# Inverse roots on VectorE instead of ScalarE, and small products moved into a bank of scores

## The chip, the cores and the metric

The kernel runs on one core of one Trainium2 chip. The metric is the device time of one execution in microseconds (us). All data is float32.

## The reference

The input is `x` of 8 images, 256 channels, 64 x 64 pixels. Two layers are applied, each on a group-normalised `x` (32 groups of 8 channels, mean and variance over the group's channels and all pixels) and each added to `x`:

```python
def _gn(v, G=32, eps=1e-5):
    g = v.reshape(B_, G, C_ // G, H_, W_)
    m = jnp.mean(g, axis=(2, 3, 4), keepdims=True)
    s = jnp.var(g, axis=(2, 3, 4), keepdims=True)
    return ((g - m) / jnp.sqrt(s + eps)).reshape(v.shape)
x = x + layer0(_gn(x))
x = x + layer1(_gn(x))
```

Layer 0 makes three 1x1 convolutions, runs two of them through batch norms, ReLUs and two more 1x1 convolutions to nine weights per pixel and group, and sums the third over a 3x3 neighbourhood with those weights. Layer 1 is half an attention over a 7x7 neighbourhood in 4 heads (with a position term and softmax) and half a sum of nine depthwise convolutions weighted by a softmax over nine. An inverse square root is needed once for the batch norms and twice for each image, for the group norm of each layer.

## The kernel before

An image is cut into 8 bands (i = 0 to 7) of 8 rows. A loop over `g` (64 bands of layer 1) has 8 steps `s` in each turn. A turn computes layer 1 on band `g`, and beside it layer 0 on band `g + 12`, so that TensorE, VectorE (DVE), ScalarE (ACT) and GpSimd (POOL) all work through a queue of instructions whose order is written out by hand under `tc.manual_schedule()`. Twelve turns with `g < 0` come first; they have layer 0 alone.

In each step the function `advance()` is called six times, and `after(n, f)` puts `f` behind the n-th call from now. I call these places 1 to 6 of a step:

- Before place 1: in even steps the scores of two tiles of the attention (L736, into the tile `sco`), the weighted values of the steps before (L785, into the tile `small`) and a transpose (`ptp`, L773). In every step then `masked` (VectorE, L750, reads `sco`, writes the negative maximum `nmax`), `add_values` (L804) and the exponentials (ScalarE, L758).
- Between places 1 and 2: the first product `pf` of the convolution weights (L872) with its exponential `ex` (L877), in odd steps a transpose, and two depthwise taps on VectorE (L829 or L855).
- Between 2 and 3: `probabilities` (VectorE L765, ScalarE L767) and the matmuls of `mid`: queries (L670), keys (L692), values (L594) or layer 0's maps (L369).
- Between 3 and 4: what follows these matmuls. For keys that is the additions L700 and L707 on VectorE; in step 3 of most bands they belong to the second half of the channels, of which the scores of step 4 are made. Then more taps.
- Between 4 and 5: the second `pf` and `ex`. Between 5 and 6: `end`, among it layer 0's tap weights `pw` (L464), whose products on VectorE (L477) come one and two places later and are added up on GpSimd (L485). GpSimd also adds the two `ex` (L1087).

TensorE's results are in eight banks of 512 columns: a score tile takes two (one per head of a pair; a step pair uses 2 x 196 = 392 columns of each), `small` one, `acc` one, and the other four rotate under the tag `gen`, one bank for each tile, however narrow.

`small` is shared: weighted values are written to its columns 0 to 255 (`po = home[:, : 2 * P]`), and layer 0's small maps (L328) or hidden products (L428) to columns from 256 on (`p12 = home[:, 2 * P :]`).

The group norms are done by `gn_affine`, a chain of functions a1 to a6 that follow each other by `after`. Per-channel means and variances come from `bn_aggr`; a first small matmul (L237) averages the means over each group (`pg`), a2 (L246, L249, L250) turns that into `d`, a second matmul averages `d`, and from that come the scale `sc` (inverse root) and the shift `bi` (L269). It is used twice:

- `scaled_weights` (below: event a), called in step 2 of the band i = 3, for the layer 0 of the next image. It scales the weights on ScalarE (`scale`, L296 and L297) and makes bias products `pb` (`through`, L304) that `biases` adds up.
- `norm_rows` (event b), called in step 2 of the band i = 6, for the layer 1 of the next image. It copies scale and shift (`keep`), spreads them over channels by four small matmuls (`by_channel`, L542, tile `pgc`), and `take` (L547) copies the result.

For images 0 and 1 (event a) and 0 (event b) this is in the turns with `g < 0`; six events a and seven events b are in the turns with `g >= 0`. The last event b is in a turn with no layer 0 beside it.

In terms of step and place, event a goes: a1 at 2/3, a2 at 2/5, a3 at 3/4, a4 (L258) at 3/6, a5 (the square root on ScalarE, L262) at 4/2, a6 and `scale` at 4/6, `through` at 5/5, `biases` at 6/1. Event b is the same up to a6 with `keep`; `by_channel` follows at 5/3 and `take` at 5/5.

Of the kernel before, what the change touches and what calls it, by code (L numbers as in the profile page):

```python
# [9 lines left out]

F32 = mybir.dt.float32
BF16 = mybir.dt.bfloat16
AF = mybir.ActivationFunctionType
ALU = mybir.AluOpType
AX = mybir.AxisListType
# [3 lines left out]
P = 128  # L19
C = 256  # L20
NCT = C // P
# [5 lines left out]
GN_EPS = 1e-5  # L27
BN_EPS = 1e-5
# [26 lines left out]
NKEY = KW * KW  # L55
CHUNK = R * KW
NPROB = 2 * CHUNK
NEG = -1.0e30


AHEAD = NB + 4
# [25 lines left out]
def conv_layers_kernel(ctx: ExitStack, tc: tile.TileContext, ins: dict, out: bass.AP):  # L87
    nc = tc.nc
# [3 lines left out]
    const = ctx.enter_context(tc.tile_pool(name="const", bufs=1))  # L92
# [14 lines left out]
    def load(name, shape, src=None, now=True):  # L107
        t = const.tile(shape, F32, name=f"c_{name}")
        late.append(lambda: nc.scalar.dma_start(out=t, in_=ins[name] if src is None else src))
        if now:  # L110
            late.pop()()
        return t

    gmat = load("gmat", [P, P])
    par = load("par", [P, NPAR])
# [24 lines left out]
    for t in probs + x3n + h2n:  # L140
        nc.gpsimd.memset(t, 0.0)

    def rstd_(out_, var, eps):
        nc.vector.tensor_scalar(out_, var, eps, None, ALU.add)
        nc.scalar.activation(out_, out_, AF.Sqrt)
        nc.vector.reciprocal(out_, out_)


    bn1s = const.tile([P, 3], F32, name="bn1s")
    bn1b = const.tile([P, 3], F32, name="bn1b")  # L150
    bn2s = const.tile([P, 1], F32, name="bn2s")
    bn2b = const.tile([P, 1], F32, name="bn2b")
    for s, t, g, b_, m, v, n, p in (
        (bn1s, bn1b, PG, PB, PM, PV, 3, P),
        (bn2s, bn2b, PG2, PB2, PM2, PV2, 1, P),
    ):
        rstd_(s, par[:p, v : v + n], BN_EPS)
        nc.vector.tensor_mul(s, s, par[:p, g : g + n])
        nc.vector.tensor_mul(t, s, par[:p, m : m + n])
        nc.vector.tensor_sub(t, par[:p, b_ : b_ + n], t)  # L160
# [19 lines left out]
    stat = ctx.enter_context(tc.tile_pool(name="stat", bufs=2))  # L180
    w0 = ctx.enter_context(tc.tile_pool(name="l0", bufs=2))
    w1 = ctx.enter_context(tc.tile_pool(name="l1", bufs=2))
    ps = ctx.enter_context(tc.tile_pool(name="ps", bufs=1, space=PSUM))
# [31 lines left out]
    def after(n, f):  # L215
        later.append((place[0] + n, f))

    def advance():
# [3 lines left out]
        for f in ready:  # L222
            f()

    def gn_affine(sts, means, name, done):


        n = len(sts)
        mv = stat.tile([P, n, 2], F32, name=f"mv_{name}", tag=f"mv{n}")
        for ct, st in enumerate(sts):  # L230
            nc.vector.bn_aggr(mv[:, ct, :], st)
        mean, var = mv[:, :, 0], mv[:, :, 1]
        gm, d, sc, bi = (stat.tile([P, n], F32, name=f"{v}_{name}", tag=f"{v}{n}") for v in ("gm", "d", "sc", "bi"))

        def group_means(v, k):
            pg = ps.tile([P, n], F32, name=f"pg_{name}_{k}", tag="gen", bufs=4)
            nc.tensor.matmul(pg, means, v, start=True, stop=True)  # L237
            return pg


        def a1():
            pg = group_means(mean, 0)
            after(2, lambda: a2(pg))

        def a2(pg):
            nc.vector.tensor_copy(gm, pg)  # L246
            for ct in range(n):
                c = slice(ct, ct + 1)
                nc.vector.tensor_scalar(d[:, c], pg[:, c], mean[:, c], None, ALU.subtract)  # L249
                nc.vector.tensor_scalar(d[:, c], d[:, c], d[:, c], var[:, c], ALU.mult, ALU.add)  # L250
            after(5, a3)

        def a3():
            pg = group_means(d, 1)
            after(2, lambda: a4(pg))

        def a4(pg):
            nc.vector.tensor_scalar(sc, pg, GN_EPS, None, ALU.add)  # L258
            after(2, a5)

        def a5():
            nc.scalar.activation(sc, sc, AF.Sqrt)  # L262
            after(4, a6)

        def a6():
            nc.vector.reciprocal(sc, sc)
            for ct in range(n):
                c = slice(ct, ct + 1)
                nc.vector.tensor_scalar(bi[:, c], gm[:, c], sc[:, c], -1.0, ALU.mult, ALU.mult)  # L269
            done(sc, bi)  # L270

        after(3, a1)


# [13 lines left out]
    def scaled_weights(b):  # L288

        im = images[b]  # L290

        def scale(sc, bi):
            im.w12s = w0.tile([P, NCT, 2 * REL], F32, tag="w12s", name=f"w12s_{b}", bufs=1)
            im.w3s = w0.tile([P, NCT, C], F32, tag="w3s", name=f"w3s_{b}", bufs=1)
            for kt in range(NCT):
                nc.scalar.activation(im.w12s[:, kt], w12[:, kt], AF.Copy, scale=sc[:, kt : kt + 1])  # L296
                nc.scalar.activation(im.w3s[:, kt], w3[:, kt], AF.Copy, scale=sc[:, kt : kt + 1])  # L297
            after(5, lambda: through(bi))

        def through(bi):  # L300
            pb = ps.tile([P, 1 + NCT], F32, tag="gen", name=f"pb_{b}", bufs=4)
            for m, to, w in ((0, 0, w12), (0, 64, w12), (1, 0, w3[:, :, :P]), (2, 0, w3[:, :, P:])):
                for kt in range(NCT):
                    nc.tensor.matmul(  # L304
                        pb[to : to + w.shape[2], m : m + 1], w[:, kt], bi[:, kt : kt + 1],
                        start=(kt == 0), stop=(kt == NCT - 1),
                    )
            after(2, lambda: biases(pb))

        def biases(pb):  # L310
            im.bias = w0.tile([P, 1 + NCT], F32, tag="bias", name=f"bias_{b}")
            nc.vector.tensor_add(im.bias[:, 0:1], pb[:, 0:1], par[:, PB21 : PB21 + 1])
            for ct in range(NCT):
                nc.vector.tensor_add(
                    im.bias[:, 1 + ct : 2 + ct], pb[:, 1 + ct : 2 + ct], chan[:, ct, CB3 : CB3 + 1]
                )

        gn_affine([im.st0[:, ct] for ct in range(NCT)], gmat, f"a{b}", scale)

    def small_maps(b, i, home):  # L320
# [208 lines left out]
    def norm_rows(b):  # L529
        im = images[b]  # L530


        def keep(sc, bi):
            both = stat.tile([P, 2], F32, name=f"both_{b}", tag="both")
            nc.vector.tensor_copy(both[:, 0:1], sc)
            nc.vector.tensor_copy(both[:, 1:2], bi)
            after(3, lambda: by_channel(both))

        def by_channel(both):
            pg = ps.tile([P, NCT, 2], F32, tag="gen", name=f"pgc_{b}", bufs=4)  # L540
            for ct in range(NCT):
                nc.tensor.matmul(pg[:, ct], gc[:, ct], both, start=True, stop=True)  # L542
            after(2, lambda: take(pg))

        def take(pg):
            im.aff = stat.tile([P, NCT, 2], F32, name=f"aff_{b}", tag="aff")
            nc.vector.tensor_copy(im.aff, pg)  # L547

        gn_affine([im.st1], gq, f"b{b}", keep)
# [174 lines left out]
    def score_tile(nm):  # L724

        return ps.tile([P, 2, 512], F32, tag="sco", name=f"sco_{nm}")
# [66 lines left out]
    def small_tile(nm):  # L793

        return ps.tile([P, 4 * P], F32, tag="small", name=f"small_{nm}")
# [214 lines left out]
    with tc.manual_schedule():  # L1010

        for i, use in enumerate(("xc", "xc", "xr", "xr", "xs", None, None, None)):
            t = None
            if use is None:
                t = w1.tile([P, NCT, RP, W], F32, tag="yp", name=f"x_{i}", bufs=3)
                t = t.rearrange("p t r c -> p t (r c)")[:, :, :BAND]
# [15 lines left out]
        for g in range(-AHEAD, B * NB):  # L1032
            b, i = divmod(g, NB)
            for s in range(STEPS):
# [3 lines left out]
                if g >= 0:  # L1038
                    nm = f"{b}_{i}_{ct}_{m}"
                    weighted = []  # L1040
                    if m % 2 == 0:
                        sco = score_tile(nm)
                        for e in range(2):
                            scores(b, i, ct, m + e, sco)
                        small = small_tile(nm)
                        weighted, pending = weigh_steps(pending, small), []
                        if s == 0 and g + AHEAD < B * NB:
                            mid.append(small_maps(*divmod(g + AHEAD, NB), small))
                        if s in (4, 6) and convs:
                            convs.pop()(small)  # L1050
                        if before is not None:
                            pending.append((before[:-1], transposed(nm, before[-1])))
                    prob, nmax = masked(nm, m, sco)
                    for a, po in weighted:
                        add_values(*a, po)
                    tot = exponentials(nm, prob, nmax)
# [52 lines left out]
def _layout(inputs):  # L1109
# [81 lines left out]
```

## Time and profile before

| | |
|---|---|
| Time, median of 3 runs | 3910.43 us (3908.52 to 3914.09) |
| Profiled execution | 3911.49 us, its span 3909.7 us |
| TensorE clock granted | 0.994 |
| First product of layer 1 (`pf`) at | 236.9 us |
| ScalarE: Exp of weights `ex`, L877 | 1024 times, 588 ns |
| ScalarE: Sqrt in `gn_affine`, L262 | 16 times, 0.2 us |
| ScalarE: table loads | 28, each 1283 ns |
| VectorE: `masked`, L750 | 1024 times, 354 ns |
| VectorE: products of tap weights, L477 | 576 times, 1286 ns |
| GpSimd: their additions, L485 | 549 times, 2184 ns |

A line of the profile names the source line, the engine, the operation, the tile that is written and those that are read, and the tile's partitions x elements. PEld is TensorE's loading of weights, beside its matmuls. A timeline gives start and duration of an instruction in us, the chain of waits gives start and length of the pieces that, followed back from the end, released each other. The time of a step is read from the first `pf` of one step to the first `pf` of the next. In plain bands (i = 1, 2, 4) the eight steps together take 57.6 us, in the bands with event a 60.36 us, in those with event b 57.8, in i = 7 62.8 and in i = 0 59.5.

### The profile page before, as it was taken

The numbers are of one execution on the slowest core, as the hardware profiler recorded it, in microseconds if no ns is written. First come the engines' busy times: TensorE is split into PE (matmuls) and PEld (weight loads), VectorE is DVE, ScalarE is ACT, GpSimd is POOL, SyncE is SP. The second block draws the span as 40 slices with busy tenths as digits, with TensorE's granted clock in tenths as the row PEclk, the third lists the DMA queues.
The fourth block names the chain that finished last, engine by engine and source line by source line (L and its number), as shares of the span: only waits on it lengthen the run. The fifth ranks groups of instructions, "written<-read, shape, count | busy, mean of one in ns | idle before, by whom it ended". The sixth has DMA issues, their size and how long they took to land.

```text
span 3909.7 us, 71679 instructions
## 1 busy us (share of the span) xinstructions
PE 3778.1 (97%) x24620; PEld 2112.2 (54%) x24620; DVE 3419.7 (87%) x7143; ACT 2835.8 (73%) x6779; POOL 3172.5 (81%) x2156
## 2 busy tenths in 40 slices
PE   5889999999999999999999999999999999999998
PEld 2445555555555555555555555555555555555554
DVE  6879898899898999899998998989988889978778
ACT  4457777777777777777777777777777777677776
POOL 4768888888887988888888888978988888956665
PEclk9999999999999999999999999999999999999999
DMA  8764443543444543543444443444433443322221
GB/s 245 208 168 128 127 118 115 143 121 116 124 123 123 142 118 105 140 131 114 139 111 128 136 119 113 127 138 116 130 111 100 133 122 94 87 85 79 72 60 35
DMA packets 429710, 473.36 MB, mean 121 GB/s; under 512 B 60992, under 2 KB 322208, under 8 KB 429088
## 3 DMA queue, kind: packets, MB, share of 16 engines
q1 hardware_dynamic: 412768, 453.01, 41.1%
q10 hardware_dynamic: 16576, 15.76, 1.3%
q8 instruction: 194, 3.18, 0.3%
q14 instruction: 172, 1.41, 0.1%
HBM read 329.08 MB, written 143.00 MB: 121 GB/s over the span
## 4 chain that ended last, share of the span: by engine, by line
PE 41%; DVE 24%; POOL 15%; ACT 11%; issue 6%; DMA 3%; SPq 0%; ACTq 0%; POOLq 0%; DVEq 0%
PE pf L872 19%; POOL xg L485 8%; DVE prod L477 7%; DVE acc L855 5%; DVE rec L893 5%; POOL ex L1087 4%; PE small L785 3%; PE pv L594 3%; ACT x L343 3%; PE ptp L773 3%; PE sco L736 3%; PE pk L692 2%; PE pq L670 2%; ACT ex L877 2%; DMA x<-x3n 2%
## 5 line engine op out<-in xcount | busy, mean ns | idle before, releaser
L872 PE MATMUL pf<-yp,c_wfc 128*128 128x512 f32 x4096 | 1916.6, 594 | 17.8 <-ACT ex L877 6.8
L485 POOL TENSOR_TENSOR xg<-xg,prod 128x1024 f32<-128x1024 f32 x549 | 1198.8, 2184 | 106.7 <-DVE prod L477 82.5
L872 PEld LDWEIGHTS pf<-yp,c_wfc 128*128 128x128 f32 x4096 | 738.5, 190 | 719.0 <-issue 629.2
L1087 POOL TENSOR_TENSOR ex<-ex,ex 128x1024 f32<-128x1024 f32 x384 | 908.2, 2365 | 66.4 <-ACT ex L877 62.5
L829 DVE SCALAR_TENSOR_TENSOR acc<-yp,c_chan,acc 128x504 f32<-128x504 f32 (+3 forms) x1104 | 775.4, 702 | 64.7 <-ACT acc L820 41.3
L477 DVE SCALAR_TENSOR_TENSOR prod<-pw,c_par,x3q 128x1040 f32<-128x1040 f32 x576 | 737.0, 1286 | 103.6 <-PE pw L464 57.4
L855 DVE SCALAR_TENSOR_TENSOR acc<-hid,c_chan,acc 128x504 f32<-128x504 f32 (+3 forms) x1024 | 750.6, 733 | 18.1
L877 ACT ACTIVATE ex<-pf 128x512 f32<-128x512 f32 x1024 | 602.0, 588 | 214.5 <-PE pf L872 197.5
L758 ACT ACTIVATE prob<-prob,nmax 128x196 f32<-128x196 f32 x1024 | 459.1, 451 | 224.5 <-DVE nmax L750 224.3
L767 ACT ACTIVATE prob<-prob,tot 128x196 f32<-128x196 f32 x1024 | 413.1, 452 | 249.5 <-DVE tot L765 248.3
L894 POOL TENSOR_TENSOR tot<-tot,rec 128x256 f32<-128x256 f32 x254 | 185.4, 730 | 398.0 <-DVE rec L893 391.6
L893 DVE RECIPROCAL rec<-tot 128x256 f32<-128x256 f32 x256 | 445.8, 1742 | 9.5 <-POOL tot L894 4.3
L775 ACT COPY pt<-ptp 112x512 f32<-112x512 f32 x511 | 295.0, 577 | 110.3 <-PE ptp L773 109.9
L750 DVE CUSTOM_DVE_ANT_0 prob<-sco,c_mask 128x196 f32<-128x196 f32 x1024 | 324.4, 354 | 28.1 <-PE sco L736 28.0
L773 PEld LDWEIGHTS ptp<-ident,prob 128*112 128x112 f32 x2044 | 227.2, 133 | 184.2 <-issue 157.1
L773 PE MATMUL ptp<-ident,prob 128*112 128x128 f32 x2044 | 319.0, 279 | 0.0
L785 PEld LDWEIGHTS small<-pt,vt 112*64 112x64 f32 x8144 | 258.2, 137 | 77.4 <-issue 75.7
L785 PE MATMUL small<-pt,vt 112*64 112x64 f32 x8144 | 293.7, 225 | 1.2 <-DMA vt<-vd 1.2
L369 PE MATMUL p<-xc,w3s 128*128 128x512 f32 x512 | 248.3, 608 | 15.8 <-ACT ex L877 15.8
L594 PE MATMUL pv<-c_wv,yp 128*128 128x256 f32 x1056 | 252.1, 381 | 7.4 <-ACT qb L674 6.0
L888 POOL TENSOR_SCALAR tot<-tot 128x512 f32<-128x512 f32 x127 | 243.6, 1918 | 11.1
L464 PEld LDWEIGHTS pw<-h2n,c_c 128*128 128x128 f32 x1152 | 176.2, 192 | 137.6 <-issue 122.7
(139 smaller groups left out, 4750.0 us busy)
## 6 DMA issues: line engine op xcount, KB each, us to landing
vt<-vd SPq DMA_DIRECT2D x512, 112.0 KB
x3q<-x SPq DMA_DIRECT2D x128, 264.0 KB
xc<-in_x SPq DMA_DIRECT2D x64, 512.0 KB
xg<-in_xg SPq DMA_DIRECT2D x64, 512.0 KB
yp<-x SPq DMA_DIRECT2D x128, 256.0 KB
xr<-x SPq DMA_DIRECT2D x64, 512.0 KB
out_x<-xr SPq DMA_DIRECT2D x64, 512.0 KB
xs<-in_x SPq DMA_DIRECT2D x57, 512.0 KB
```

What stands on the lines that cost most here:

```text
L477: nc.vector.scalar_tensor_tensor(prod[:, :, :RUN], pw[:, j, :RUN].unsqueeze(1).to_broadcast([P, SHARE, RUN]), par[:, PCB2 + k : PCB2 + k + 1],
L485: nc.gpsimd.tensor_add(im.xg[i], im.xg[i], rows(prod))
L758: nc.scalar.activation(prob[:, h, :NKEY], prob[:, h, :NKEY], AF.Exp, bias=nmax[:, h : h + 1], scale=-1.0, accum_out=tot[:, h : h + 1],)
L767: nc.scalar.activation(prob[:, h, :NKEY], prob[:, h, :NKEY], AF.Copy, scale=tot[:, h : h + 1])
L773: nc.tensor.transpose(ptp[:, h, ch], prob[:, h, ch * CHUNK : (ch + 1) * CHUNK], ident)
L785: nc.tensor.matmul(po[half[h], :, t * TQ : (t + 1) * TQ], im.vt[i + ch, m][:n, t, (2 * ct + h) * HD : (2 * ct + h + 1) * HD], pt[:n, h, ch ...
L829: nc.vector.scalar_tensor_tensor(o, yp[:, ct, ra + dr : rb + dr, ca + dc : cb + dc], chan[:, ct, CW1 + k : CW1 + k + 1], o, ALU.mult, ALU.add,
L855: nc.vector.scalar_tensor_tensor(o, hid[:, ra + dr : rb + dr, ca + dc : cb + dc], chan[:, ct, CW2 + k : CW2 + k + 1], o, ALU.mult, ALU.add,)
L872: nc.tensor.matmul(pf, wfc[:, kt, 2 * m + j, ct * P : (ct + 1) * P], images[b].yp[i][:, kt, PAD : PAD + R], start=(kt == 0), stop=(kt == N ...
L877: nc.scalar.activation(ex[:, j].rearrange("p (r c) -> p r c", r=R), pf, AF.Exp)
L893: nc.vector.reciprocal(rec, v)
L1087: after(4, lambda ex=ex, exb=exb: nc.gpsimd.tensor_add(ex, ex, exb))
```

## The change

The inverse roots are no longer made by Sqrt on ScalarE and a reciprocal on VectorE, but on VectorE alone: from the bits of the number, shifted right by one and taken from a constant, comes a first guess, and three Newton steps of three instructions follow. With the addition of eps these are 12 instructions for each root. The functions a5 and a6 go into a4.

The small products are no longer tiles of their own under `gen`. Once there is a score tile (`g >= 0`), `narrow` gives them columns behind the 392 in use, in the first bank of the latest score tile: 0 and 4 for the two products of `group_means`, 8 for `pb`, 12 for `pgc`. The distances in `after` change too. In step and place, event a now goes: a1 at 2/3, a2 at 2/4, a3 at 3/1, a4 with the roots and `scale` at 3/2, `through` at 4/1, `biases` at 4/2. Event b: the same up to a4 with `keep`, `by_channel` at 4/1, `take` at 4/2.

```diff
+ROOT = float(0x5F3759DF)
...
-    def rstd_(out_, var, eps):
-        nc.vector.tensor_scalar(out_, var, eps, None, ALU.add)
-        nc.scalar.activation(out_, out_, AF.Sqrt)
-        nc.vector.reciprocal(out_, out_)
+    def rstd_(out_, var, eps, v, t):
+
+        bits = out_.bitcast(I32)
+        nc.vector.tensor_scalar(v, var, eps, None, ALU.add)
+        nc.vector.tensor_scalar(bits, v.bitcast(I32), 1, None, ALU.logical_shift_right)
+        nc.vector.tensor_scalar(bits, bits, -1.0, ROOT, ALU.mult, ALU.add)
+        for _ in range(3):
+            nc.vector.scalar_tensor_tensor(t, out_, -0.5, out_, ALU.mult, ALU.mult)
+            nc.vector.tensor_mul(t, t, v)
+            nc.vector.scalar_tensor_tensor(out_, t, 1.5, out_, ALU.add, ALU.mult)
...
+    beside_scores = []
+
+    def narrow(name, at, n):
+
+        if not beside_scores:
+            return ps.tile([P, n], F32, tag="gen", name=name, bufs=4)
+        return beside_scores[-1][:, 0, 2 * NKEY + at : 2 * NKEY + at + n]
+
...
         def group_means(v, k):
-            pg = ps.tile([P, n], F32, name=f"pg_{name}_{k}", tag="gen", bufs=4)
+            pg = narrow(f"pg_{name}_{k}", 4 * k, n)
             nc.tensor.matmul(pg, means, v, start=True, stop=True)
             return pg
...
             pg = group_means(mean, 0)
-            after(2, lambda: a2(pg))
+            after(1, lambda: a2(pg))
...
-            after(5, a3)
+            after(3, a3)
 
         def a3():
             pg = group_means(d, 1)
-            after(2, lambda: a4(pg))
+            after(1, lambda: a4(pg))
 
         def a4(pg):
-            nc.vector.tensor_scalar(sc, pg, GN_EPS, None, ALU.add)
-            after(2, a5)
-
-        def a5():
-            nc.scalar.activation(sc, sc, AF.Sqrt)
-            after(4, a6)
-
-        def a6():
-            nc.vector.reciprocal(sc, sc)
+            rstd_(sc, pg, GN_EPS, va, d)
...
         def through(bi):
-            pb = ps.tile([P, 1 + NCT], F32, tag="gen", name=f"pb_{b}", bufs=4)
+            pb = narrow(f"pb_{b}", 8, 1 + NCT)
...
-            after(2, lambda: biases(pb))
+            after(1, lambda: biases(pb))
...
-            after(3, lambda: by_channel(both))
+            after(5, lambda: by_channel(both))
 
         def by_channel(both):
-            pg = ps.tile([P, NCT, 2], F32, tag="gen", name=f"pgc_{b}", bufs=4)
+            pg = narrow(f"pgc_{b}", 12, NCT * 2).rearrange("p (t n) -> p t n", t=NCT)
...
-            after(2, lambda: take(pg))
+            after(1, lambda: take(pg))
...
                         sco = score_tile(nm)
+                        beside_scores[:] = [sco]
```

More of the change, by code (lines that the diff above doesn't have):

```diff
@@ L11 @@
 F32 = mybir.dt.float32
-BF16 = mybir.dt.bfloat16
+I32 = mybir.dt.int32
 AF = mybir.ActivationFunctionType
@@ L141, in conv_layers_kernel @@
         nc.gpsimd.memset(t, 0.0)
-    def rstd_(out_, var, eps):
-        nc.vector.tensor_scalar(out_, var, eps, None, ALU.add)
-        nc.scalar.activation(out_, out_, AF.Sqrt)
-        nc.vector.reciprocal(out_, out_)
+    def rstd_(out_, var, eps, v, t):
[7 more added lines that the diff above has]
+            nc.vector.scalar_tensor_tensor(out_, t, 1.5, out_, ALU.add, ALU.mult)
+    root = [const.tile([P, 3], F32, name=f"root_{i}") for i in range(2)]
     bn1s = const.tile([P, 3], F32, name="bn1s")
@@ L156, in conv_layers_kernel @@
     ):
-        rstd_(s, par[:p, v : v + n], BN_EPS)
+        rstd_(s, par[:p, v : v + n], BN_EPS, root[0][:p, :n], root[1][:p, :n])
         nc.vector.tensor_mul(s, s, par[:p, g : g + n])
@@ L232, in gn_affine @@
         mean, var = mv[:, :, 0], mv[:, :, 1]
-        gm, d, sc, bi = (stat.tile([P, n], F32, name=f"{v}_{name}", tag=f"{v}{n}") for v in ("gm", "d", "sc", "bi"))
+        gm, d, sc, bi, va = (stat.tile([P, n], F32, name=f"{v}_{name}", tag=f"{v}{n}") for v in ("gm", "d", "sc", "bi", "va"))
         def group_means(v, k):
-            pg = ps.tile([P, n], F32, name=f"pg_{name}_{k}", tag="gen", bufs=4)
+            pg = narrow(f"pg_{name}_{k}", 4 * k, n)
             nc.tensor.matmul(pg, means, v, start=True, stop=True)
```

## The prediction

> **What bounds the kernel now.** I read the page's busy times first, then the widths of bands with and without the changed steps, then the chain of waits through one changed band, and the timelines of TensorE and VectorE around it. A change under 0.2% (8 us) can't be told from none here.
>
> ```profile
> PE 3778.1 (97%) x24620; PEld 2112.2 (54%) x24620; DVE 3419.7 (87%) x7143; ACT 2835.8 (73%) x6779; POOL 3172.5 (81%) x2156
> ```
>
> TensorE has 131.6 us idle in the span of 3909.7, and slice by slice most of it is before the first image of layer 1 (236.9 us). From there a time can only fall by what stalls TensorE, so I compare two bands by windows: a plain one (i=2 of the second image, 831.6 to 889.2) and the next, where the group statistics for layer 0 are taken (889.2 to 949.5).
>
> ```profile
> 831.60:889.20 57.60, 57.25 (x381) 32.06 (x380) 52.39 (x108) 43.31 (x104) 50.57 (x35) 1.00 0.44 127
> 889.20:949.50 60.30, 59.27 (x400) 33.55 (x399) 54.30 (x121) 47.13 (x111) 52.88 (x37) 1.00 0.45 127
> ```
>
> The columns are the width, then busy PE, PEld, DVE, ACT, POOL. The second is 2.7 us longer: 2.02 are its own small matmuls, and TensorE's idle time is 1.03 against 0.35. So 1.03 us is all that a perfect change can win in such a band. The chain of waits tells whose it is:
>
> ```profile
> 909.29 0.75 DVE acc L855
> 910.04 0.06 DVE gm_a L246
> ...
> 912.18 0.27 DVE prob L750
> ...
> 914.02 0.38 PE pg_a L237 x2
> ...
> 916.69 0.92 PE sco L736 x15
> ...
> 921.57 1.73 PE pv L594 x8
> 923.29 1.72 PE pf L872 x4
> 925.01 0.45 PE pw L464 x4
> ```
>
> Until 914 the chain runs on VectorE, which is behind TensorE here; after that on TensorE. ScalarE's two table loads of this band (922.56 and 925.41) lie where the chain is all TensorE: nothing waits for them.
>
> **What is taken away.** The Sqrt activations go, and with them the table loads:
>
> ```profile
> L262 ACT ACT_TABLE_LOAD x13 | 16.7, 1283 | 0.2
> L877 ACT ACT_TABLE_LOAD x13 | 16.7, 1283 | 0.2
> ```
>
> That is 26 x 1.283 = 33 us of ScalarE, or 2.8 us per event with the Sqrt itself, for 13 events: six "a" events (layer 0's statistics, i=3) and seven "b" events (layer 1's, i=6). On the path it is worth 0 by the chain above. What hides it is TensorE's own work at 921 to 931; were ScalarE the bound there, it would be worth the 33 us.
>
> The Trainium skill (ScalarE: Activation LUTs, What ACT_TABLE_LOAD costs) adds a drain and puts a switch at about 2.66 us, so 26 switches would be an estimated 69 us. The trace shows 1.30 us from the load's start (922.56) to the Sqrt (923.86), with no such drain; neither figure moves the sum, since both are covered.
>
> The small products also leave the four rotating banks. Stalls by them: TensorE waited 0.83 us before the second `pg_a` (914.02), 0.38 before `pg_b` (1089.36), and 0.76 at 1104.06 behind `pgc`. These go, at least where they are.
>
> **What the new places do: event a.** The second product (a3) moves from place 4 of step 3 to place 1 of step 3. The timelines:
>
> ```profile
> 908.70 0.61 PE L464 MATMUL pw<-h2n,c_c 128*128 128x132 f32 x4
> 909.15 1.88 PE L872 MATMUL pf<-yp,c_wfc 128*128 128x512 f32 x4
> ```
> ```profile
> 910.70 0.27 DVE L250 TENSOR_SCALAR d_a<-d_a,mv_a 128x1 f32<-128x1 f32 x1
> ...
> 912.10 0.35 DVE L750 CUSTOM_DVE_ANT_0 prob<-sco,c_mask 128x196 f32<-128x196 f32 x1
> ...
> 915.30 0.16 DVE L765 RECIPROCAL tot<-tot 128x2 f32<-128x2 f32 x1
> 915.37 0.73 DVE L700 SCALAR_TENSOR_TENSOR kb<-pk,c_chan,pe 128x512 f32<-128x512 f32 x1
> 916.02 0.52 DVE L707 SCALAR_TENSOR_TENSOR kb<-pk,c_chan,pe 128x16 f32<-128x16 f32 x3
> ```
>
> TensorE would reach the new place at 909.13, after `pw` and before `pf`. Its operand `d` is ready at 910.97 (910.70 + 0.27): a2 is only renumbered, from place 5 to 4, and no VectorE work stands between. The target bank is worse: step 3's `masked` is issued before place 1 and reads that bank until 912.45. Do waits go by bank or by column? This row of `add_values`, which reads columns 0 to 255 of `small`, shows the program waiting for writes to columns 256 to 511:
>
> ```profile
>   PE small L328: 16.4, 26
> ```
>
> So I take by bank: the product starts at 912.53 and `pf` at 912.77, 3.62 us later than now. Up to the second `pf` it regains the stall and slot of the old place (pk to pf 2.96 now, 1.72 without): 3.62 - 1.24 = 2.38 us late. By column it starts at 911.03 and 2.38 becomes 0.9.
>
> The Trainium skill (PSUM — Partial Sum Buffer, PSUM bank collisions raise a hardware error) says the same against this change: guard by bank and quadrant, not by address, disjoint columns included. By it TensorE's route is 2.38, by addresses 0.9; the L328 row already picked the first.
>
> The second route is VectorE. The roots (a4) now stand at place 2 of step 3, ahead of `L765` and of the key additions L700 and L707, for which step 4's scores wait (L707 ends at 916.54, scores start at 916.69). Before, that place held nothing. The Newton chain is 3 + 3 x 3 = 12 tiny instructions, each needing the one before. No such chain is in the trace. Bounds: tiny independent ones start 0.07 us apart (909.95, 910.02), so 12 x 0.07 = 0.8; the slowest dependent pair (L250, 0.27 plus a 0.03 gap) gives 12 x 0.30 = 3.6. The nearest are the 0.15 us immediates (L258) plus the 0.03 us gap seen from L249 to L250: 12 x 0.18 = 2.2, and 0.35 for the two `bi`. So 2.55 us ahead of the keys, and scores start 2.5 us late. Two routes, 2.4 and 2.5, side by side and not added: 2.55 us per event (ends 0.9, where waits go by column and the chain takes 0.8, and 4.0, a chain of 3.6 with its two `bi`).
>
> Behind the waiting product stand on TensorE `pf`, `ptp`, the keys and the scores; behind the roots on VectorE, L765, on which ScalarE's L767 and then the second `ex` wait, and GpSimd's L1087 behind that (now 918.37, idle some 2 us). The four scalings on ScalarE (1.28 us, 927.20 to 928.48) move forward past oc, hid, acc and the next exponentials to stand ahead of L767; `ex` ends near 920.2 instead of 916.86, still before the bank is asked for at about 925. The 16 `pb` matmuls (1.34 us, 931.00 on) only move to step 4, where VectorE's `masked` has ended by then. The scalings now overwrite weights that step 1's L369 reads last, so they wait for nothing new. Some 0.5 us of VectorE's small work leaves step 4 and 0.3 us of `biases` comes to it from step 6; VectorE has that much room there (0.56 us idle at 925.55). No DMA moves. Later bands pass the delay on, as VectorE waits for TensorE again in each of them.
>
> Six a events: 6 x 2.55 = 15.3 us.
>
> **Event b.** The same two routes: the product waits for `masked` until 1087.79 instead of following `pw` at 1084.9: `pf` 3.17 late, less (2.51 - 1.72): 2.4; VectorE carries two copies more, 2.65. Then the 0.76 us at 1104.06 falls away: 2.55 - 0.76 = 1.8. But from 1081 to 1129 GpSimd is busy without a break and VectorE's product at 1109.58 waits for it (0.92 us). GpSimd is set back only by the later L1087, some 0.7 us. So the delay at that point lies between 0.7 and 1.8: I take 1.2, the middle, for six events: 7.2 (ends -0.3 each, a 0.9 as in event a less the stalls of 0.38 and 0.76, and 3.6, a slow chain and no cover). The seventh (i=6 of the last image) has no layer 0 beside it; TensorE at 3424.1 waits for `masked` until 3425.7: 1.7 (ends 0 and 2.5).
>
> **Before the first scores** the products keep their own banks. Image 0's root lies on the path: L258 at 24.31 to ScalarE at 24.94 is 0.63, the Newton chain 2.2, so +1.6. Image 1's `pb` (148.93, 2.32 us, on the chain) no longer waits for a Sqrt queued behind a DMA and can fall into TensorE's idle time: up to -2.3. The first Exp's load at 238.54 (1.28, on the chain) goes if the first table chosen holds Exp. Image 0's second chain stands ahead of a product that GpSimd wants: up to +1.8. The signs cancel; I take 0 (ends -4 and +4). The batch norm roots, about 24 instructions before 12 us, lie where VectorE waits for DMAs (5.02, 1.18, 0.87, 1.08 us).
>
> **Sum.** 15.3 + 7.2 + 1.7 + 0 = 24.2 us. The profiled execution took 3911.49 us (1.8 outside its span); 3935.7, and as the median 3910.43 is 1.06 below it, **3934.6 us**.
>
> **Rivals.**
> - *Faster: stalls go and nothing takes their place.* VectorE is at `masked` before TensorE reaches place 1. Then 6 x 0.83 + 6 x (0.38 + 0.76) = 12 us less: 3898.6. For: ScalarE and the banks are relieved. Against: VectorE would have to be 3.3 us further on (912.45 against 909.13), and it is 87% busy. The crossing point is a VectorE lag of about 0.8 us there, the stall removed. Chance 0.10.
> - *No change.* Waits go by column and the chain runs at the independent rate: 6 x 0.9 + 6 x -0.3 + 0 = 3.6 us, 3914. Against: the L328 row. Chance 0.08.
> - *Slower still.* The chain takes 3.6 us, and GpSimd covers nothing: 6 x 4.0 + 6 x 3.6 + 2.5 + 4 = 52, 3962. Chance 0.06 for over 3952.
> - *It doesn't do what it says*: some loads stay. As they are hidden this moves nothing, and the forecast stands.
>
> **How the numbers follow.** The forecast has 0.76, the upper rival 0.06: slower 0.82. Faster 0.10, same 0.08. The range reaches from 3912, which leaves the first rival and half of the second below, to 3952, above which only the third lies.
>
> **What would show it.** Right: two table loads at most; in each i=3 band, `pg_a<-d_a` with TensorE idle some 3 us before it, released by L750; step 2 of these bands, from `pf` to `pf`, near 9.4 us instead of 5.83 and step 5 near 8.8 instead of 10.12 (`pb` gone from it); the twelve Newton rows near 0.18 us apart, ahead of L765; the band at 62.9 instead of 60.36. Wrong: `pg_a<-d_a` starting at d's end (waits by column), keys not later than now (the chain is covered), i=3 bands under 60.3, or i=6 and i=7 bands together longer by over 2 us (GpSimd covers nothing).

## The result and the profile after

The changed kernel takes 4026.38 us (median of 5 runs, 4024.04 to 4027.11) against 3910.43 (3908.52 to 3914.09): the ratio is 1.0294, with a 95% interval from 1.0279 to 1.0309. That is 116 us slower; 24 were forecast, 3952 was the upper end. The direction was right and the size was wrong.

Line numbers have moved: `masked` is L757 now, the second product and the first both L252, the chain of roots L147 to L153, `bi` L276, the key additions L707 and L714, the scores L743, `pf` L879, `ex` L884, the additions of tap products on GpSimd L492 and of two `ex` L1095. Small products show as writing to `sco`.

First the page's busy times, then what TensorE waited for (us in total, times, longest):

```profile
PE 3821.4 (95%) x24620; PEld 2138.6 (53%) x24620; DVE 3502.9 (87%) x7323; ACT 2813.5 (70%) x6734; POOL 3176.4 (79%) x2156
```
```profile
PE sco L252 <- DVE nmax L757: 40.9, 13, 3.5
PE sco L743 <- DVE kb L714: 39.9, 42, 4.5
```

The span grew by 114.9 us. TensorE is busy 43.3 us longer with the same 24620 matmuls, so these became slower, and it is idle 71.6 us longer. The first wait is the forecast one, for `masked`, 3.15 us for each of 13 events. The second, scores waiting for keys, was 5.2 us in all before (29 times, 0.2 us at most):

```profile
PE sco L736 <- DVE kb L707: 5.2, 29, 0.2
```

The next view has the same two bands as before, by windows:

```profile
859.10:916.70 57.60, 57.22 (x381) 31.98 (x379) 52.33 (x107) 43.36 (x104) 50.57 (x35) 1.00 0.45 127
916.70:985.56 68.86, 62.41 (x401) 35.41 (x399) 60.25 (x131) 45.28 (x108) 53.31 (x37) 0.95 0.40 112
```

The plain band is unchanged. The band with event a takes 68.86 instead of 60.3, VectorE is busy 6 us more in it, and the granted clock (0.95, third column from the end) shows the slower matmuls. Over the whole kernel, counted from `pf` to `pf`, the i=3 bands are longer by 56.1 us and the i=6 bands by 49.8; i=0 by 1.0, the others by 0.5 at most; 6.3 come before the first `pf` of layer 1. The chain of waits through event a tells what lasts so long:

```profile
943.97 2.03 DVE d_a L151
...
946.03 2.28 DVE d_a L152
...
948.33 0.17 DVE sc_a L153
...
951.34 1.59 PE sco L743 x16
```

Two of the twelve tiny instructions take over 2 us, L148 takes 0.69 (the timeline below has it), the rest 0.17 at most, and the chain from 942.85 to 949.66 takes 6.8 us where 2.2 were forecast. The timeline shows GpSimd beside them:

```profile
941.54 4.44 POOL L492 TENSOR_TENSOR xg<-xg,prod 128x1024 f32<-128x1024 f32 x2
943.04 0.69 DVE L148 TENSOR_SCALAR sc_a<-va_a 128x2 int32<-128x2 int32 x1
943.97 2.02 DVE L151 SCALAR_TENSOR_TENSOR d_a<-sc_a 128x2 f32<-128x2 f32 x1
945.94 2.33 POOL L1095 TENSOR_TENSOR ex<-ex,ex 128x1024 f32<-128x1024 f32 x1
946.03 2.27 DVE L152 TENSOR_TENSOR d_a<-d_a,va_a 128x2 f32<-128x2 f32 x1
948.33 0.16 DVE L153 SCALAR_TENSOR_TENSOR sc_a<-d_a,sc_a 128x2 f32<-128x2 f32 x1
```

GpSimd's two L492 end at 943.71 and 945.98, its L1095 at 948.27. VectorE's three long instructions end at 943.73, 945.99 and 948.29. From then until 953.99 GpSimd has nothing to do, and the rest of the chain runs through. In the whole trace 39 of the 192 instructions of the 16 chains for group norms last over 0.3 us, and all 39 end within 0.03 us of the end of a GpSimd instruction. In event b, where the operands have one column, L148 and L149 (one operand) are never long; at 1127 to 1133 us L151 (0.74 and 2.27) and L153 (2.02), which read two from SBUF, are.

The matmuls slow down after idle time, as the windows before and after the wait for `masked` show:

```profile
936.00:940.30 4.30, 0.87 (x5) 0.43 (x4) 4.19 (x14) 2.47 (x5) 4.16 (x4) 1.00 0.00 0
940.30:944.20 3.90, 3.85 (x8) 1.67 (x9) 3.76 (x7) 0.75 (x4) 3.81 (x3) 0.57 0.45 142
```

TensorE is idle for 3.5 us up to 940.35; then the granted clock is 0.57, and the four `pf` matmuls take 3.56 us instead of 1.88. The same follows the idle 2.76 us before the scores.

### The profile page after: what moved, and what is told of

The parts are those of the page before. It is cut to its first block, busy times and chain, and to the rows that moved or that the text cites. A ratio compares the mean times of both kernels' runs of the same rounds, so it can differ in the third digit from the quotient of the medians.

```text
span 4024.6 us, 71787 instructions
## 1 busy us (share of the span) xinstructions
PE 3821.4 (95%) x24620; PEld 2138.6 (53%) x24620; DVE 3502.9 (87%) x7323; ACT 2813.5 (70%) x6734; POOL 3176.4 (79%) x2156
## 4 chain that ended last, share of the span: by engine, by line
PE 43%; DVE 28%; POOL 11%; ACT 9%; issue 5%; DMA 2%; ACTq 0%; SPq 0%; DVEq 0%; POOLq 0%
PE pf L879 20%; DVE prod L484 7%; POOL xg L492 6%; DVE acc L862 6%; DVE rec L900 5%; PE small L792 4%; PE pv L601 4%; PE ptp L780 3%; PE sco L743 3%; POOL ex L1095 3%; ACT x L350 3%; PE pk L699 3%; PE pq L677 2%; DVE acc L836 2%; DMA x<-x3n 2%
## 5 line engine op out<-in xcount | busy, mean ns | idle before, releaser
L879 PE MATMUL pf<-yp,c_wfc 128*128 128x512 f32 x4096 | 1931.4, 598 | 12.0 <-DVE prod L484 6.6
L492 POOL TENSOR_TENSOR xg<-xg,prod 128x1024 f32<-128x1024 f32 x549 | 1200.9, 2187 | 196.7 <-DVE prod L484 169.1
L879 PEld LDWEIGHTS pf<-yp,c_wfc 128*128 128x128 f32 x4096 | 741.8, 191 | 721.7 <-issue 641.2
L1095 POOL TENSOR_TENSOR ex<-ex,ex 128x1024 f32<-128x1024 f32 x384 | 908.0, 2364 | 75.3 <-ACT ex L884 72.4
L884 ACT ACTIVATE ex<-pf 128x512 f32<-128x512 f32 x1024 | 603.7, 590 | 258.7 <-PE pf L879 241.8
L757 DVE CUSTOM_DVE_ANT_0 prob<-sco,c_mask 128x196 f32<-128x196 f32 x1024 | 324.7, 355 | 24.7 <-PE sco L743 24.7
L792 PEld LDWEIGHTS small<-pt,vt 112*64 112x64 f32 x8144 | 266.8, 141 | 83.1 <-issue 78.0
L792 PE MATMUL small<-pt,vt 112*64 112x64 f32 x8144 | 302.8, 229 | 4.5 <-DMA vt<-vd 4.5
L743 PE MATMUL sco<-kb,qb 64*64 64x196 f32 x4096 | 240.3, 349 | 43.0 <-DVE kb L714 39.9
L895 POOL TENSOR_SCALAR tot<-tot 128x512 f32<-128x512 f32 x127 | 243.8, 1920 | 11.1
```

The lines of the kernel that those rows point to most:

```text
L492: nc.gpsimd.tensor_add(im.xg[i], im.xg[i], rows(prod))
L792: nc.tensor.matmul(po[half[h], :, t * TQ : (t + 1) * TQ], im.vt[i + ch, m][:n, t, (2 * ct + h) * HD : (2 * ct + h + 1) * HD], pt[:n, h, ch ...
L879: nc.tensor.matmul(pf, wfc[:, kt, 2 * m + j, ct * P : (ct + 1) * P], images[b].yp[i][:, kt, PAD : PAD + R], start=(kt == 0), stop=(kt == N ...
L884: nc.scalar.activation(ex[:, j].rearrange("p (r c) -> p r c", r=R), pf, AF.Exp)
L1095: after(4, lambda ex=ex, exb=exb: nc.gpsimd.tensor_add(ex, ex, exb))
```

## Experiments

Theory H: an instruction of VectorE that reads two operands from SBUF (or a `tensor_scalar` of two columns within SBUF) is held while a GpSimd instruction runs. Rival F: these instructions are slow by themselves. Theory S: the wait for `masked` and the chain ahead of the keys stand side by side, so that only the longer counts. The times are medians; the ratio is to the kernel before, run on the same chip.

Builds differ before the first `pf` of layer 1 by some us even where the code there is the same, so differences under 5 us between two experiments are not read, and the table at the end counts from that `pf`.

**One operand from SBUF (e1_one_sbuf).** The intermediate `t` goes to a PSUM column, the square is made column by column with a pointer:

```diff
-            rstd_(sc, pg, GN_EPS, va, d)
+            if beside_scores:
+                one_sbuf_(sc, pg, GN_EPS, va, narrow(f"work_{name}", 20, n))
+            else:
+                rstd_(sc, pg, GN_EPS, va, d)
...
+    def one_sbuf_(y, var, eps, v, t):
+        nc.vector.tensor_scalar(v, var, eps, None, ALU.add)
+        nc.vector.tensor_scalar(t.bitcast(I32), v.bitcast(I32), 1, None, ALU.logical_shift_right)
+        nc.vector.tensor_scalar(y.bitcast(I32), t.bitcast(I32), -1.0, ROOT, ALU.mult, ALU.add)
+        for _ in range(3):
+            for c in range(y.shape[1]):
+                o = slice(c, c + 1)
+                nc.vector.tensor_scalar(t[:, o], y[:, o], y[:, o], -0.5, ALU.mult, ALU.mult)
+            nc.vector.tensor_mul(t, t, v)
+            nc.vector.scalar_tensor_tensor(y, t, 1.5, y, ALU.add, ALU.mult)
```

Expected: 

> From layer 1 on, the Newton chain keeps its intermediate in a PSUM column, so that none of its instructions reads two operands from SBUF, and the shift of two columns writes to PSUM; per Newton step the square becomes one instruction per column (15 instructions for event a, 12 for b). Theory H (an instruction with two SBUF operands, or the two-column shift, is held while GpSimd runs): no instruction of the chain over 0.35 us, chain 3.1 us (15 x 0.2) instead of 6.8 in event a and 2.4 instead of 6.2 in b; keys ready near 1.2 us after pk; the scores of step 4 start right behind pw, at 8.2 us after the product of place 1 instead of 11.0; 4.2 us saved per event (2.8 idle, 1.4 of half pace behind it), 12 events: 50 us, 3976. The wait of TensorE for masked (3.5 us idle) and the half pace of the pf behind it stay. Rival F (the long instructions are slow for themselves, by their place in a fresh stretch of code or by the int32 form, whatever GpSimd does): two or three instructions of 2 us stay, and 3 more instructions cost 0.6 us: 4026 to 4034.

Measured: 3972.57 us (ratio 1.0152, 1.0135 to 1.0169). The timeline of VectorE in event a:

```profile
937.45 0.17 DVE L164 TENSOR_TENSOR sco<-sco,va_a 128x2 f32<-128x2 f32 x1
941.13 0.75 DVE L722 SCALAR_TENSOR_TENSOR kb<-pk,c_chan,pe 128x512 f32<-128x512 f32 x1 [1.05 <-PE pk L714]
```

In the events beside layer 1 no instruction of the chain lasts over 0.23 us, though 158 of them run from start to end beside a single GpSimd instruction. In event a the chain takes 3.3 us, and the keys now wait for TensorE's `pk`, not the scores for the keys (5.6 us in all). The scores start 9.3 us after the product instead of 11.0 (8.2 were expected, but TensorE stays at half pace longer here: `pk`, which takes 1.88 us after the change, takes 2.38). F falls; H stands with 54 us of the 116. The wait for `masked` stayed (40.8 us).

**GpSimd silent (e9_quiet).** The counter-test leaves the chain and takes GpSimd's work away:

```diff
+                quiet[0] = g >= 0 and g % 8 in (3, 6) and s in (2, 3)
...
-            else:
+            elif not quiet[0]:
                 nc.gpsimd.tensor_add(im.xg[i], im.xg[i], rows(prod))
...
-                    if exb is not None:
+                    if exb is not None and not (quiet[0] and s == 2):
```

Expected: 

> The changed kernel, its Newton chain untouched, with GpSimd's work beside the chain left out: in the bands i=3 and i=6 the additions of tap products in steps 2 and 3 and the addition of two ex after step 2 are not done (their part of the sums is missing). Counter-test to e1_one_sbuf, which changed the chain and left GpSimd. Theory H: with nothing running on GpSimd no instruction of the chain is over 0.3 us, 12 x 0.195 = 2.3 us, keys ready before TensorE asks for them; the wait for masked and its half pace stay: as e1_one_sbuf, 3965 to 3976. Rival F (the chain's own instructions are slow): 4020 or more.

Measured: 3984.09 us (1.0180, 1.0165 to 1.0195). The same instructions as after the change, in event a:

```profile
937.03 0.16 DVE L151 SCALAR_TENSOR_TENSOR d_a<-sc_a 128x2 f32<-128x2 f32 x1
941.18 0.75 DVE L708 SCALAR_TENSOR_TENSOR kb<-pk,c_chan,pe 128x512 f32<-128x512 f32 x1 [1.99 <-PE pk L700]
```

In the events where GpSimd was silent no instruction of the chain lasts over 0.17 us; the 12 take 2.3 us. Only two are long in the whole trace, both before layer 1, where GpSimd was left at work. The time is 8 us over the expected range. From the first `pf` on, the profile is 62.5 us longer than before the change (e1_one_sbuf: 60.3), as H has it; 10.6 come before that `pf`, more than in any other build, and why is not known. H is shown from both sides.

**An own bank (e2_own_bank), and both edits (e3_both).**

```diff
-            pg = narrow(f"pg_{name}_{k}", 4 * k, n)
+            if k:
+                pg = ps.tile([P, n], F32, tag="gen", name=f"pg_{name}_{k}", bufs=4)
+            else:
+                pg = narrow(f"pg_{name}_{k}", 4 * k, n)
```

Expected: 

> Only the second product of the group means goes back into a bank of its own under gen; the rest is as after the change. It no longer waits for masked. If TensorE's route and VectorE's chain stand side by side (theory S): TensorE starts the product when d is ready, 1.8 us earlier, its idle time before it falls from 3.5 to 1.7 us and the clock behind it stays at 1.0, but the chain still ends where it did and the scores of step 4 wait for the keys: the idle time turns up there, 6 us instead of 2.8. Total within 5 us of 4026, less the 1.7 of the last event b. Rival A (the two waits add up, each with its stretch of half pace): 12 x (1.8 + 1.7) = 42 us less, 3984.

Measured: 4026.79 us (1.0296, 1.0280 to 1.0311). TensorE's waits:

```profile
PE sco L746 <- DVE kb L717: 73.8, 42, 5.7
```

The wait for `masked` is gone. The product still waits 1.81 us for `d` in each event a beside layer 1, and the scores wait 73.8 us in all instead of 39.9. S holds: while the chain is held, the forecast's first route costs nothing.

Expected: 

> The edits of e1_one_sbuf and e2_own_bank together. Theory H with S: no wait for masked and no held instruction; what is left is the chain of 3.1 (a) or 2.4 us (b) and the bi ahead of the keys, as the prediction had it: keys ready at about 7.4 us after masked's end, TensorE idle some 2.3 us before the scores of step 4, band i=3 longer by 3 to 4 us than before the change instead of 8.6: 3964 (3950 to 3976). If this is no faster than e1_one_sbuf by over 4 us, the wait for masked costs nothing once the chain is short.

Measured: 3964.77 us (1.0135, 1.0120 to 1.0150), as S had it. By accident this build also prices the half pace. Two of its six i=3 bands take 65.43 us and four 63.96, with the same instructions and the same idle 2.06 us ahead of the scores. The windows of that idle time and of what follows, in a short band and in a long one:

```profile
933.01:935.07 2.06, 0.00 (x1) 0.03 (x1) 1.97 (x10) 1.64 (x6) 2.06 (x2) 1.00 0.97 371
935.07:937.00 1.93, 1.93 (x48) 1.57 (x48) 1.89 (x3) 1.52 (x5) 0.46 (x1) 1.00 1.12 286
```
```profile
1410.26:1412.29 2.03, 0.00 (x0) 0.00 (x1) 1.94 (x10) 1.62 (x5) 2.03 (x2) 1.00 0.99 371
1412.30:1414.20 1.90, 1.88 (x28) 1.34 (x30) 1.86 (x3) 1.49 (x4) 0.48 (x1) 0.59 1.15 305
```

The clock is 1.00 in one and 0.59 in the other, 28 matmuls come through instead of 48, and the band is 1.47 us longer. So one stretch of half pace costs about 1.5 us, and after 2.06 us of idle time it comes or doesn't (the last section says when). In the changed kernel it came after 23 of the 24 idle times of 2.7 us or more beside layer 1.

**Other places (e4_late, e5_late_own, e7_early).** The product at 3/4 and the roots at 3/6, behind the keys:

```diff
-            after(3, a3)
+            after(6, a3)
...
-            after(1, lambda: a4(pg))
+            after(2, lambda: a4(pg))
```

Expected: 

> The change with other places: the second product at 3/4 and the roots at 3/6, where they stood before the change; Newton chain, banks and all else as after it. The product has no masked to wait for, and the chain stands behind the keys. Theory: the holds by GpSimd stay (same long instructions, each ending with a GpSimd instruction), but nothing that TensorE wants next stands behind them; VectorE gets 5 to 7 us later once per event and takes it back over the band (5.2 us of room in 57.6): 0 to 3 us per event, 12 events, less 6 x 0.83 + 6 x 1.14 of stalls that go, plus 6 of the turns before layer 1: 3930 (3904 to 3950). Rival V (VectorE's time counts wherever it is lost): 12 x 6.5 = 78 us, 3990 or more.

Measured: 3953.52 us (1.0108, 1.0092 to 1.0123), above the range and far below V's 3990. The timeline shows a wait that I hadn't foreseen, of step 4's scores for the addition of eps, which reads the product from the one buffer of the score tile:

```profile
929.04 0.92 PE L743 MATMUL sco<-kb,qb 64*64 64x196 f32 x16 [1.74 <-DVE va_a L147]
```

e5_late_own gives that product a bank of its own again (the edit of e2_own_bank on top).

Expected: 

> As e4_late, but the second product of the group means has a bank of its own under gen, and so the addition of eps behind it reads no bank of scores. In e4_late the scores of step 4 waited 1.72 us for that addition, since the score tile has one buffer. Theory W (the bank, held by the late reader, is what e4_late lost): 1.7 us per event come back, 12 events: 3953.5 - 20.6 = 3933; of the rotating banks' old stalls up to 6 x (0.83 + 0.38) may return: 3933 to 3940. Rival L (scores wait for VectorE's lateness in general): no gain, 3950 to 3956.

Measured: 3950.34 us (1.0106, 1.0089 to 1.0123). The wait is gone and the time is the same; my sum (W) fails. The timeline of step 4:

```profile
929.67 2.36 POOL L1098 TENSOR_TENSOR ex<-ex,ex 128x1024 f32<-128x1024 f32 x1
929.77 2.28 DVE L149 TENSOR_SCALAR sc_a<-sc_a 128x2 int32<-128x2 int32 x1
933.85 0.35 ACT L306 ACTIVATE w12s<-c_w,sc_a 128x64 f32<-128x64 f32 x1 [3.07 <-DVE sc_a L153]
935.75 1.99 PE L882 MATMUL pf<-yp,c_wfc 128*128 128x512 f32 x4 [1.17 <-ACT pt L785]
```

The held chain (929.19 to 933.8) now stands ahead of step 4's `masked`, and ScalarE is held with it. In event a its four scalings stand behind the chain: ScalarE is idle 3.07 us for the roots, and the copy `pt`, which comes after the scalings, is what the next `pf` waits 1.17 us for. In event b ScalarE's exponentials wait for `masked` (4.07 us, at 1113.32). In event a's band step 4 is 2.87 us longer. In e7_early the product stands at 3/3 in the scores' bank, and only the addition of eps is ahead of the keys:

```diff
-            after(3, a3)
+            after(5, a3)
...
             pg = group_means(d, 1)
-            after(1, lambda: a4(pg))
+            nc.vector.tensor_scalar(va, pg, GN_EPS, None, ALU.add)
+            after(3, a4)
```

Expected: 

> As after the change, with the second product at 3/3 in the scores' bank and the addition of eps issued right behind it, ahead of the keys; the rest of the chain (11 instructions, two operands from SBUF) at 3/6, behind them. By then masked has long read the bank, and the scores of step 4 find their bank read early. Theories H, S and W together: no wait for masked, none of the scores for the addition, 0.2 us ahead of the keys, no stall of the rotating banks: 3953.5 - 12 x 1.7 + 12 x 0.2 = 3935, 5 less where e5_late_own pays the old stalls. If the keys are late by over 0.5 us, the product after pk is waited for on VectorE.

Measured: 3951.79 us (1.0107, 1.0092 to 1.0122), 17 us above what was expected and the same as e5_late_own, with the same waits (ScalarE 2.99 us for the roots, `pf` 1.10 us for `pt`).

**Late and not held (e6_late_own_one).** e5_late_own with the chain of e1_one_sbuf, `t` in the second half of the product's own bank.

Expected: 

> As e5_late_own, with the chain of e1_one_sbuf (one operand from SBUF, the other in the product's own bank), in the turns before layer 1 too. Tells what the holds by GpSimd cost when the chain stands behind the keys. If VectorE's room hides them (theory C): within 4 us of e5_late_own, less 2 to 3 us before the first scores. If they count (rival V): 12 x 3 to 4 us less than e5_late_own, 40 us.

Measured: 3930.14 us (1.0052, 1.0037 to 1.0067): 20 us less than e5_late_own, midway between the theories. VectorE hides some of the holds, not all. Against the kernel before, an i=3 band is still 0.86 us longer and an i=6 band 1.1 to 1.2 (once 1.5).

**What was taken away (e10_no_sqrt, e8_sqrt_narrow).** Both start from the kernel before.

```diff
-            nc.scalar.activation(sc, sc, AF.Sqrt)
+            nc.scalar.copy(sc, sc)
```

Expected: 

> The kernel before, with the square root in gn_affine replaced by a copy on ScalarE at the same place (the scale is then 1/(variance + eps)): 26 of the 28 table loads go, with the Sqrt, and nothing else changes. What the loads were worth on the path. The prediction's step (covered by TensorE's work, worth 0): 3906 to 3914. Rival (ScalarE's 33 us count): down to 3877.

Measured: 3911.96 us against 3912.56 (0.9997, 0.9987 to 1.0006), with 2 table loads left. The 26 others were worth nothing, as predicted. In e8_sqrt_narrow the Sqrt stays:

```diff
-            after(5, a3)
+            after(4, a3)
...
-            after(2, lambda: a4(pg))
-
-        def a4(pg):
             nc.vector.tensor_scalar(sc, pg, GN_EPS, None, ALU.add)
-            after(2, a5)
+            after(5, a5)
...
-            after(2, lambda: take(pg))
+            take(pg)
```

Expected: 

> The kernel before, with Sqrt on ScalarE and its 28 table loads, but with the second product of the group means at 3/3 and the products pgc in the scores' bank, each read right behind the product. Nothing of the Newton chain. What the rotating banks' stalls were worth: 6 x (0.83 + 0.38 + 0.76) = 11.8 us less 13 x 0.2 ahead of the keys: 3901. If the stalls are late on TensorE only because VectorE is behind there (the chain of waits of before ran on VectorE until 914), they turn up at the next wait and the time stays at 3910.

Measured: 3910.65 us against 3910.35 (1.0002, 0.9993 to 1.0012). The stall was not the product's:

```profile
913.07 1.98 PE L880 MATMUL pf<-yp,c_wfc 128*128 128x512 f32 x4 [0.72 <-ACT ex L885]
```

ScalarE's `ex` was what held the next bank under `gen`; now `pf` asks for it and waits 0.72 us where `pg_a` had waited 0.83. The i=3 bands take 60.43 us, as before (60.36).

**Taken together**, from the first `pf` of layer 1 to the end, us over the kernel before, by the profiled executions:

| Place of the roots | chain held | chain not held |
|---|---|---|
| 3/2, product waits for `masked` | 108.6 (the change) | 60.3 (e1_one_sbuf), 62.5 (e9_quiet) |
| 3/2, product in its own bank | 106.7 (e2_own_bank) | 43.7 (e3_both) |
| 3/6, product in its own bank | 33.5 (e5_late_own) | 13.1 (e6_late_own_one) |

The profiled execution of e1_one_sbuf was the slowest of its runs, 8 us over the median, so its entry may be that much too high; the others lie within 3 us of their medians. No version with the new roots came below the kernel before. With the loads and the stalls worth nothing there is nothing for the new roots to win here.

## Why the prediction was wrong, and where it was right

- **The failed step is the length of the chain, "12 x 0.18 = 2.2".** The unit price was good: instructions that nothing holds start 0.195 us apart (12 take 2.3). But the rows that I took it from read one operand from SBUF or none, and most of the chain reads two. With GpSimd at work it took 6.8 us, outside even my upper bound of 3.6. It set the band: from the end of `masked` (its second instruction) to the scores it took 3.95 us before (912.74 to 916.69) and 11.05 after (940.29 to 951.34), 7.1 more; scores and weighted values at half pace took (1.59 + 1.87) - (0.92 + 1.15) = 1.4 more; that is the band's 8.5.
- **The trace of before had the row.** Before layer 1 one weight is subtracted from the others (L200), in two instructions of equal size with two operands in SBUF; the group's mean of 3241 ns joins 4.20 and 2.28 us. The timeline of VectorE and GpSimd:

```profile
54.19 4.43 POOL L485 TENSOR_TENSOR xg<-xg,prod 128x1024 f32<-128x1024 f32 x2
...
56.57 4.20 DVE L200 TENSOR_TENSOR c_wfc<-c_wfc,last 128x2048 f32<-128x2048 f32 x1
...
72.53 2.28 DVE L200 TENSOR_TENSOR c_wfc<-c_wfc,last 128x2048 f32<-128x2048 f32 x1
```

  The first stood from 56.57 until GpSimd ended at 58.62 and then took its 2.15 us; beside the second GpSimd was idle (71.81 to 76.17). The Trainium skill (SBUF — State Buffer, Who interferes with whom) says as much: a VectorE instruction with two SBUF inputs, or one in a two-port mode, shares a port pair with GpSimd, whole instruction against whole instruction. The traces agree, with 39 of 39 long instructions of the changed kernel ending with GpSimd's (one case that differs stands in the last section). I had weighed a rule on banks, and not this one, which spoke louder against the change.
- **No term for TensorE's pace.** I counted an idle 3 us as 3 us. Each stretch of half pace behind such an idle time cost about 1.5 us more, in nearly every event twice; 40.7 of TensorE's 43.3 us of longer work lie in the i=3 and i=6 bands. The chain's length alone does not make up the miss: with a chain of 2.3 us, as the sum had it (e9_quiet), an i=3 band is still 5.4 us longer instead of 2.55 and an i=6 band 4.8 instead of 1.2. There TensorE's own route sets the band: `pf` starts 4.1 us late behind the wait for `masked`, what comes from there to `pk` takes 2.3 us more at half pace, and about 1 us is regained before the scores. Here, too, the trace of before had a row, after an idle 1.94 us at the start of layer 1:

```profile
244.50:246.40 1.90, 0.01 (x1) 0.01 (x1) 1.10 (x2) 1.81 (x5) 0.60 (x4) 1.00 0.44 129
246.40:248.50 2.10, 2.10 (x4) 0.86 (x5) 0.54 (x2) 2.10 (x7) 0.00 (x0) 0.67 0.85 250
```

- **The wait for `masked`** came as forecast, not by column, released by L757, 3.48 us idle (3.4 by the forecast's times), step 2 at 9.72 (9.4). It goes by the whole score tile, not by bank: in all 13 events the product starts 0.05 us after the second instruction of `masked`, which reads the tile's other bank, and 0.34 after the first, which reads the product's:

```profile
939.65 0.35 DVE L757 CUSTOM_DVE_ANT_0 prob<-sco,c_mask 128x196 f32<-128x196 f32 x1
...
939.93 0.36 DVE L757 CUSTOM_DVE_ANT_0 prob<-sco,c_mask 128x196 f32<-128x196 f32 x1
...
940.35 0.38 PE L252 MATMUL sco<-d_a,c_gmat 128*128 128x2 f32 x2 [3.48 <-DVE nmax L757]
```

  The forecast took the end of the first (912.45; the second ends at 912.74), and this is the 0.3 us between 9.4 and 9.72. That the two routes don't add up was right as well (e2_own_bank). Alone, with its half pace, the wait is worth 17 us (e1_one_sbuf against e3_both), or 8 by the medians.
- **The stalls that "go"** went, for another reason than mine. In the changed kernel `pk` to `pf` takes 1.72 us (944.53 to 946.25), as forecast, and the waits of `pf` and the small products for `ex` fall from 14.1 us in 21 events (6.8, 5.0 and 2.3) to 2.3 in 3. But moving the product frees nothing by itself: in e8_sqrt_narrow, where TensorE isn't late, `pf` waits 0.72 us for the same `ex`. So the credit of 1.24 us held because TensorE comes later, and the faster rival's 12 us were never there to win.
- **Table loads worth 0** was right (e10_no_sqrt); one is left after the change. Step 5 fell to 8.69 (8.8 forecast).
- **Event b**: 1.2 forecast, 8.0 measured. GpSimd was no cover; it was what held the chain. My own mark for this, i=6 and i=7 together longer by over 2 us, was hit. The last event b cost 2.6 (1.7 forecast).
- **Before the first scores**: 0 forecast (-4 to +4), 6.3 measured, 4.4 to 10.6 over the nine builds with Newton steps, against -2.6 and +2.1 in e10_no_sqrt and e8_sqrt_narrow. In image 1's event a TensorE waits 3.46 us at the earlier place for `d`, and L149 is held 2.05 us; in image 0's event b the product for the channels waits 1.51 us behind a held L151 (1.93). How the 6.3 divide between place and holds was not tried.
- **Left open**: the 13.1 us of e6_late_own_one. VectorE's 12 to 15 instructions per event are the likely cause, and in event a ScalarE's scalings, which still wait 1.79 us for the roots (at 929.89) ahead of the exponentials; neither was tested alone.

## What to carry to other kernels

A tiny instruction is priced by the engines that run beside it, not only by its length: look in the trace for one with the same kind of operands beside a busy GpSimd, and where a group's mean joins two very different times, open it. A stall belongs to what releases it, so moving the waiting instruction away frees nothing if the next one asks for the same thing. A wait of 2 us or more on TensorE can cost more than itself, by what follows at half pace.

## What the hardware showed that I had not expected

- The chain's instructions on VectorE, 1 or 2 columns wide and 0.16 us alone, took 0.7 to 2.3 us in the changed kernel when they met GpSimd's, and ended within 0.03 us of them. This holds for two operands in SBUF and for the two-column `tensor_scalar` forms within SBUF; with one operand or the result in PSUM, or with one column and one operand, none was held. Not every GpSimd instruction holds them: in the last event b of e4_late they meet L895, which has one operand; the first (3475.63) takes 0.47 us, and the next four take 0.16 while L895 runs on to 3477.39.
- The granted clock fell, to 0.5 in the end, after idle times well under 3 us: after 1.94 us in the kernel before, in e3_both after 2.06 in two of six equal bands and after 1.81 in two of six, in e4_late after 1.75 in two of twelve, and between the first and the last `pf` in no run after 1.7 or less. The traces also say when. From layer 1 on, the stretches at 0.5 in one trace start whole multiples of 3.41 us apart and last 3.41 or 6.83 us (once 13.65, and without the one at the very end). I laid windows of 3.41 us on that grid in all twelve traces, up to the last `pf`. Where TensorE ran no matmul for 2.02 us or more of a window at full clock, the next window ran at 0.5 (65 of 65); with 1.75 to 2.01 us it did so 9 times of 15, with less never. So an idle time counts by how much of it falls into one window. In e3_both, all of the 2.06 us before 1412.32 lay in 1409.24 to 1412.65, and of those before 935.07 only 1.77 lay in 931.37 to 934.78. The one idle time of 3.04 us in the changed kernel that cost nothing (up to 3075.65) was split into 1.54 and 1.50. The Trainium skill (TensorE: Matmul & The Clock Gate, Part 1) gives a window of about 3.4 us that runs freely of the kernel, and the traces agree; it has the clock drop after an idle window, and here 1.75 to 2.0 us idle in one were enough.
